# Graph layer kernel: product tiles in a new order, unused ranks taken from the row projection, edge sums joined to rank sums ahead of W2

## The chip, the cores and the metric

The kernel runs on one core of a Trainium2 chip. The metric is device time in microseconds (us) of the whole program, the median of several runs. The engines of the core work side by side: TensorE (PE in the profile; its weight loads are PEld), VectorE (DVE), ScalarE (ACT), GpSimd (POOL) and SyncE (SP), which here issues the DMA transfers. Each takes its own instructions in order and waits for others by semaphores.

## The reference

128 graphs of 128 nodes with 64 features, two layers. `h` is the layer norm of `x` with negative values set to zero.

```
mask = adj > 0
h1   = relu(h @ W1a [row j] + (h[j] - h[k]) @ W1b + b1)     # for each pair j, k; 192 hidden units
hm   = sum over k of mask[j, k] * h1[j, k, :]
x    = x + hm @ W2 + deg * b2                               # layer 0
x    = x + (adj @ h) @ W.T                                  # layer 1, h of the new x
```

With `A = h(W1a+W1b)+b1` and `C = h W1b`, one pair gives `relu(A[j] - C[k])`. The mask keeps about an eighth of the pairs, so most of the work of the dense sum is for nothing.

## The kernel before

**Tiling.** Four graphs are a group; 32 groups run one after another. The neighbours k of a row are cut in four quarters q of 32, and in each quarter a row's neighbours get ranks 0 to 5 (`D = 6`). `S` is one-hot: rank, neighbour, row. A product of the stacked projections `k3` with `S3` fetches, for each row and rank, `-C[k]`, and a second product with `id3` adds `A[j]`. The projections are split in three bf16 parts, which lie on 96 rows (3 x 32). The few neighbours beyond rank 5 of a quarter ("edges", `ov`) are gathered one by one into at most 128 edge slots (`R`, `RT`, `S2`, `X`).

The 192 hidden units are split: the first 128 (`C0`) use relu(v) = (v + |v|)/2, so DVE sums |v| straight out of PSUM into `hm0` (line 761), the linear part goes through the mask and the projections in `edge_sum`, and `w2h` is W2/2. The last 64 (`C1`) take relu on ACT into `T` (line 771), and POOL adds the 24 ranks up into `hm1` (lines 784 to 786).

**Unused ranks.** A rank that a row doesn't use fetches nothing, so its value is `A[j]` itself. What these add must be taken off again: `pre_ra` computes |A| and relu(A) with the hidden units as rows (`ra0`, `ra1`), `pre_pads` the number `np0` of used minus all ranks of each row, on all partitions, and POOL multiplies them. `edge_sum` and `edge_sum1` add the result to the edge sums (`u0`, `u1`). `post0` puts `u0`, both halves of `hm0`, `u1` and `hm1` through W2.

**Jobs.** A group takes 24 jobs, t = 0 to 23. A job fills one PSUM tile of the pool `g` (three buffers, shared with `pp` and `pr`) by products (`fill`) and drains it (`drain`): kind 0 has the first 128 units of one graph, 64 rows j (`jh`) and two quarters (`qp`), and is drained by DVE; kind 1 has the last 64 units of two graphs, one in each half of the columns, and is drained by ACT. The order is four jobs of kind 0, two of kind 1, repeated.

**What runs around the jobs.** Three tables say after which job a piece of other work is put out: `OWN` for the group of the jobs, `BEHIND` for the group before (its output), `AHEAD` for the next (its preparation). TensorE keeps this order exactly (`mm`, `tp`); within it, the other engines' instructions are placed by the framework. The pieces' small products use a second PSUM pool `m` with two buffers.

AHEAD makes, for the next group: `adjT` and `maskT` (pre_adj, t=2), the ranks `qs` (pre_rank, t=4) and from them the six planes of `S` and twelve transfers into `S3` (pre_slots, t=4), the projections `ca` and the row's part of the output `e` (pre_proj, twice), and twelve transfers of `ca` into `k3` (pre_stack). All transfers go through SP's queue in program order: `S3`, `k3`, the output of the group before, then the next loads. `S` has one buffer, `S3`, `k3` and `ca` two.

A job with `qp` 0 reads the quarters q = 0 and 1 of `S3` and `k3`, with `qp` 1 the quarters 2 and 3; q = 3 is the last one transferred.

Of the kernel before, what the change touches and what calls it, by code (L numbers as in the profile page):

```python
# [150 lines left out]
def kernel(  # L151
# [26 lines left out]
    nc = tc.nc  # L178
# [30 lines left out]
    with ExitStack() as main:  # L209
# [15 lines left out]
        ident = const.tile([P, P], F32, tag="ident", name="ident")  # L225
        make_identity(nc, ident)
        identb = const.tile([P, P], BF16, tag="identb", name="identb")
        nc.vector.tensor_copy(identb, ident)
# [12 lines left out]
        nc.vector.memset(oneb, 1.0)  # L241
        moneb = const.tile([P, P], BF16, tag="moneb", name="moneb")
        nc.vector.memset(moneb, -1.0)

# [31 lines left out]
        b1c = const.tile([P, 1], F32, tag="b1c", name="b1c")  # L276
        b1d = const.tile([P, 1], F32, tag="b1d", name="b1d")
        bias = const.tile([P, H + O], F32, tag="bias", name="bias")
        nc.vector.memset(w2bd, 0.0)
        nc.vector.memset(wl1, 0.0)  # L280
        for p in range(2):
            s = slice(p * F, (p + 1) * F)
            nc.scalar.dma_start(wa2[s, :], W1[0:F, :])
            nc.scalar.dma_start(wb2[s, :], W1[F : 2 * F, :])
            nc.scalar.dma_start(w2bd[s, p, :], W2[C0:H, :])
            nc.scalar.dma_start(wl1[s, s], W)
            nc.scalar.dma_start(b1d[s, :], b1[C0:H].unsqueeze(1))
        nc.scalar.dma_start(w2a, W2[0:C0, :])
# [137 lines left out]
        def pre_count(g):  # L426
            d = groups[g]

            pd = mtile(f"pd{g}")
            for b in range(G):  # L430
                mm(
                    pd[:, b : b + 1], d["maskT"][:, b, :], oneb[:, 0:1], start=True, stop=True
                )
                mm(
                    pd[:, G + b : G + b + 1], d["ov"][:, b, :], oneb[:, 0:1], start=True, stop=True
                )
            d["dn"] = grp.tile([P, 2, G], F32, tag="dn", name=f"dn{g}")
            nc.vector.tensor_copy(d["dn"].rearrange("j t b -> j (t b)"), pd[:, 0 : 2 * G])  # L438
            d["nb"] = tmp.tile([P, G], BF16, tag="nb", name=f"nb{g}")
            nc.vector.tensor_copy(d["nb"], d["dn"][:, 1])  # L440

        def pre_pads(g):
            d = groups[g]
            pn = mtile(f"pn{g}")
            for t, w in (("maskT", oneb), ("ov", moneb)):
                mm(
                    pn, w, d[t].rearrange("k b j -> k (b j)"), start=t == "maskT", stop=t == "ov"
                )
            d["np0"] = grp.tile([P, G, N], F32, tag="np0", name=f"np0{g}", bufs=1)
            nc.scalar.activation(  # L450
                d["np0"].rearrange("p b j -> p (b j)"), pn, AF.Copy, bias=-float(Q * D)
            )
            nc.gpsimd.tensor_tensor(d["ra0"], d["ra0"], d["np0"], ALU.mult)
            for p in range(2):
                s = slice(p * C1, (p + 1) * C1)
                nc.gpsimd.tensor_tensor(  # L456
                    d["ra1"][s], d["ra1"][s], d["np0"][s, 2 * p : 2 * p + 2], ALU.mult
                )

        def pre_proj(g, r):  # L460

            d = groups[g]
            if r == 0:

                d["ca"] = grp.tile([P, 3, 2, G, H], BF16, tag="ca", name=f"ca{g}")
                d["e"] = grp.tile([P, G, O], F32, tag="e", name=f"e{g}", bufs=3)
            pp = gtile(f"pp{g}_{r}")
# [28 lines left out]
        def pre_stack(g):  # L496
# [3 lines left out]
            for q in range(Q):  # L500
                for part in range(3):
# [3 lines left out]
                    )  # L505

        def pre_ra(g):
            d = groups[g]
            d["ra0"] = grp.tile([P, G, N], F32, tag="ra0", name=f"ra0{g}")
            d["ra1"] = grp.tile([P, 2, N], F32, tag="ra1", name=f"ra1{g}")  # L510
            halves = [slice(p * F, (p + 1) * F) for p in range(2)]
            pr = gtile(f"pr{g}")
            for p, s in enumerate(halves):
                mm(
                    pr[:, p, 0 : 2 * N].rearrange("h (r n) -> h r n", r=2),
                    wab[s, 0:C0], d["hT"][s], start=True, stop=True,
                )
            for p, s in enumerate(halves):
                mm(
                    pr[s, p, 2 * N : 4 * N].rearrange("h (r n) -> h r n", r=2),  # L520
                    wab[s, C0:H], d["hT"][s], start=True, stop=True,
                )
            nc.scalar.activation(
                d["ra0"].rearrange("h (p r) n -> h p (r n)", p=2), pr[:, :, 0 : 2 * N],
                AF.Abs, bias=b1c,
            )
            for p, s in enumerate(halves):
                nc.scalar.activation(
                    d["ra1"][s].rearrange("h r n -> h (r n)"),
                    pr[s, p, 2 * N : 4 * N], AF.Relu, bias=b1d[s],  # L530
                )

# [82 lines left out]
        def edge_sum(g):  # L615
# [3 lines left out]
            for b in range(G):  # L619
                o = ph[:, b * N : (b + 1) * N]  # L620
                mm(
                    o, d["X"][:, b, 0:C0], d["RT"][:, b, :], start=True, stop=False
                )
                for i in range(3):
# [5 lines left out]
            nc.vector.tensor_tensor(  # L630
                d["u0"], ph.rearrange("h (b j) -> h b j", b=G), d["ra0"], ALU.add
            )

        def edge_sum1(g):
            d = groups[g]
            ph = mtile(f"pe1{g}")
            for b in (0, 2, 1, 3):
                p, r = b // 2, b % 2
                mm(
                    ph[p * C1 : (p + 1) * C1, r * N : (r + 1) * N], d["X"][:, b, C0:H],  # L640
                    d["RT"][:, b, :], start=True, stop=True,
                )
            d["u1"] = tmp.tile([P, 2, N], F32, tag="u1", name=f"u1{g}", bufs=1)
            nc.vector.tensor_tensor(
                d["u1"], ph[:, 0 : 2 * N].rearrange("h (r j) -> h r j", r=2), d["ra1"], ALU.add
            )


        def post0(g):
            d = groups[g]  # L650
            py = mtile(f"py{g}")
            d["py"] = py
            for i, t in enumerate((d["u0"], d["hm0"][:, 0], d["hm0"][:, 1])):
                for p in range(2):
# [6 lines left out]
            w = w2bd.rearrange("h p o -> h (p o)")  # L661
            for i, t in enumerate(("u1", "hm1")):
                mm(
                    py[:, 0 : 2 * N], w, d[t].rearrange("h r j -> h (r j)"),
                    start=False, stop=i == 1, skip_group_check=True,
                )
            d["ys"] = tmp.tile([P, 2, N], F32, tag="ys", name=f"ys{g}")
# [50 lines left out]
        class Job:  # L718
# [108 lines left out]
        for g in range(NG):  # L827
            if g + 1 < NG:
                load(g + 1)
            for t in range(T):  # L830
# [46 lines left out]
```

## Time and profile before

| | |
|---|---|
| median of 3 runs | 1076.84 us (1076.46 to 1078.69) |
| the profiled execution | 1076.04 us, of which the span of the profile 1074.3 us |
| TensorE's granted clock | 0.987 |
| DVE: `hm` sums of kind 0 (L761) | 469.8 us busy, 949 ns each |
| POOL: sums of `T` (L784) | 442.1 us busy |
| TensorE: `g` from `S`, and from `id` | 383.4 and 381.3 us |
| ACT: `T` (L771) | 202.9 us busy, 805 ns each |
| transfers into `S3` | 384 of 192 KB, 4.0 us from issue to landing |
| transfers into `k3` | 384 of 96 KB, 2.2 us |

In the profile "out<-in" gives the tiles that an instruction writes and reads, with numbers left out: `g` are the product tiles, `pe` the sums of edge_sum and edge_sum1, `py` those of post0, `pp` the projections, `pr` and `pn` the products of pre_ra and pre_pads, `pq` the ranks, `px` the edge gather, `hm`, `u`, `T`, `S`, `k` the SBUF tiles named above. Line 181 and 184 are the helpers through which all products go, so products are told apart by their tiles. `96*64` is the shape of the weights: 96 rows, 64 columns; a number behind is the shape of the output. An fp32 product shows as two instructions. Matmuls overlap, so their durations add up to more than the time they take.

### The profile page before, as it was taken

The page shows a single profiled execution, that of the slowest core. Times are in us where ns is not written, and L with a number is a line of the kernel's source. Part 1 is how long each engine was busy: PE and PEld are TensorE (multiplying, and loading weights), DVE is VectorE, ACT ScalarE, POOL GpSimd, SP SyncE. Part 2 cuts the span into 40 slices and gives each one's busy share as a digit, 9 for nine tenths or more (in the row PEclk, how much of TensorE's full clock was granted, in tenths as well). Part 3 has the DMA queues.
Part 4 walks back from the last instruction along what each step waited for, and adds up shares of the span by engine and source line. Part 5 has one row for each costly group of instructions (what it writes and reads, how often), then busy time and mean ns, then how long its engine had stood idle before and what let it go on. Part 6 is the DMA issues. An engine that isn't in the chain of part 4 may idle for free.

```text
span 1074.3 us, 27146 instructions
## 1 busy us (share of the span) xinstructions
PE 1035.5 (96%) x10438; PEld 731.8 (68%) x10438; DVE 843.3 (79%) x1955; ACT 684.1 (64%) x1473; POOL 717.6 (67%) x810
## 2 busy tenths in 40 slices
PE   3699999999999999999999999999999999999995
PEld 1477776777677677677677677677777777667773
DVE  5468888878888878887877888877888887888763
ACT  4366666676666677666667666667666667666652
POOL 1377666777666687666686766677766677666674
PEclk9799999999999999999999999999999999999998
DMA  4456655456655456655456655445665545664420
GB/s 104 114 138 144 140 126 115 112 130 149 138 125 124 111 120 153 141 124 134 102 118 147 143 131 130 114 112 138 144 142 125 115 114 127 146 141 109 108 66 13
DMA packets 89062, 132.29 MB, mean 123 GB/s; under 512 B 47584, under 2 KB 64352, under 8 KB 88928
## 3 DMA queue, kind: packets, MB, share of 16 engines
q1 hardware_dynamic: 87552, 130.08, 53.0%
q8 instruction: 84, 1.38, 0.5%
q10 hardware_dynamic: 1376, 0.43, 0.2%
q14 instruction: 50, 0.41, 0.1%
HBM read 13.01 MB, written 4.19 MB: 16 GB/s over the span
## 4 chain that ended last, share of the span: by engine, by line
PE 93%; DVE 2%; SPq 2%; DMA 1%; ACT 1%; POOL 1%; issue 0%; ACTq 0%; POOLq 0%; DVEq 0%
PE g L181 49%; PE pe L181 7%; PE pp L181 7%; PE py L181 7%; PE px L181 6%; PE pr L181 3%; PE po L181 2%; PE pga L181 2%; PE pn L181 2%; PE pt L184 1%; PE pj L181 1%; PE pgq L181 1%; PE pq L181 1%; SPq L407 1%; DVE S L401 1%; PE pty L184 1%
## 5 line engine op out<-in xcount | busy, mean ns | idle before, releaser
L761 DVE TENSOR_REDUCE hm<-g 128x64 f32<-128x768 f32 x512 | 469.8, 949 | 115.7 <-PE g L181 113.5
L784 POOL TENSOR_TENSOR T<-T 128x768 f32<-128x768 f32 (+2 forms) x384 | 442.1, 1151 | 144.4 <-ACT T L771 126.8
L181 PEld LDWEIGHTS <-k 96*128 96x128 bf16 (+1 forms) x6144 | 408.5, 103 | 150.7 <-issue 37.2
L181 PE MATMUL g<-S,k 96*128 96x384 bf16 (+1 forms) x2048 | 383.4, 331 | 6.3 <-DMA k<-ca 5.1
L181 PE MATMUL g<-id,k 96*128 96x192 bf16 (+1 forms) x4096 | 381.3, 246 | 0.0
L771 ACT ACTIVATE T<-g 128x768 f32<-128x768 f32 x256 | 202.9, 805 | 25.4 <-PE g L181 23.4
L494 POOL TENSOR_TENSOR ca<-rest,ca 128x768 bf16<-128x768 f32 x64 | 105.0, 1642 | 170.5 <-ACT ca L493 161.1
L401 DVE TENSOR_SCALAR S<-qs 128x512 bf16<-128x512 bf16 x192 | 116.5, 675 | 3.0 <-issue 0.5
L483 ACT ACTIVATE ca<-pp 128x768 bf16<-128x768 f32 x64 | 51.3, 801 | 102.9 <-PE pp L181 99.0
L181 PE MATMUL pe<-RT,X 128*128 128x128 f32 (+1 forms) x512 | 79.4, 299 | 0.0
L493 ACT ACTIVATE ca<-rest 128x768 bf16<-128x768 f32 x64 | 53.7, 840 | 25.1 <-DVE rest L485 25.1
L181 PE MATMUL pp<-wp,hT 64*128 64x448 f32 x256 | 67.8, 607 | 1.9 <-DVE dn L438 1.9
L485 DVE TENSOR_TENSOR rest<-pp,ca 128x768 f32<-128x768 f32 x64 | 59.9, 936 | 4.5 <-ACT ca L483 4.5
L181 PEld LDWEIGHTS pe<-RT,X 128*128 128x128 f32 (+1 forms) x512 | 52.1, 164 | 9.8 <-issue 5.2
L668 ACT ACTIVATE ys<-py 128x256 f32<-128x256 f32 x32 | 12.3, 383 | 65.8 <-PE py L181 65.8
L456 POOL TENSOR_TENSOR ra<-ra,np 64x256 f32<-64x256 f32 x64 | 51.6, 806 | 2.4
L181 PE MATMUL px<-ca,S 128*128 128x192 bf16 x384 | 53.0, 247 | 0.0
L181 PE MATMUL px<-ca,R 128*128 128x192 bf16 x384 | 52.6, 246 | 0.0
L181 PEld LDWEIGHTS <-oneb 128*128 128x128 bf16 x192 | 13.5, 97 | 56.1 <-issue 56.1
L352 ACT ACTIVATE h<-x,mra,rsa 128x64 f32<-128x64 f32 x128 | 48.8, 435 | 3.7 <-DVE mra L350 2.2
L612 ACT ACTIVATE X<-px 128x256 f32<-128x256 f32 x64 | 24.5, 383 | 38.7 <-PE px L181 34.9
L181 PEld LDWEIGHTS <-R 128*128 128x128 bf16 x512 | 43.6, 98 | 7.9 <-issue 0.6
(130 smaller groups left out, 1425.0 us busy)
## 6 DMA issues: line engine op xcount, KB each, us to landing
S<-S SPq DMA_DIRECT2D x384, 192.0 KB, 4.0
k<-ca SPq DMA_DIRECT2D x384, 96.0 KB, 2.2
adj<-in_adj_dram SPq DMA_DIRECT2D x32, 256.0 KB, 2.8
x<-in_x_dram SPq DMA_DIRECT2D x32, 128.0 KB, 2.7
out_dram<-ot SPq DMA_DIRECT2D x32, 128.0 KB, 2.0
wa<-in_L_gnn_W_dram ACTq DMA_DIRECT2D x2, 48.0 KB, 2.8
wb<-in_L_gnn_W_dram ACTq DMA_DIRECT2D x2, 48.0 KB, 3.1
bias<-in_L_gnn_b_dram ACTq DMA_DIRECT2D x1, 96.0 KB, 4.1
```

What stands on the lines that cost most here:

```text
L181: return tc.keep_in_program_order(nc.tensor.matmul(*args, **kw))
L352: nc.scalar.activation(to(b), src[:, b, :], AF.Relu, bias=mr[:, b : b + 1], scale=rs[:, b : b + 1])
L401: nc.vector.tensor_scalar(d["S"][:, i, :], d["qs"].rearrange("k b j -> k (b j)"), float(i) + BIG, None, ALU.is_equal,)
L456: nc.gpsimd.tensor_tensor(d["ra1"][s], d["ra1"][s], d["np0"][s, 2 * p : 2 * p + 2], ALU.mult)
L483: nc.scalar.activation(parts[0], x, AF.Copy)
L485: nc.vector.tensor_tensor(rest, x, parts[0], ALU.subtract)
L493: nc.scalar.activation(parts[1], rest, AF.Copy)
L494: nc.gpsimd.tensor_tensor(parts[2], rest, parts[1], ALU.subtract)
L612: nc.scalar.activation(d["X"][:, r::2, 0:C0], pxv[:, :, 0:C0], AF.Abs)
L761: nc.vector.tensor_reduce(d["hm0"][:, qp, b, js], self.gt[:, :, 0:ND].rearrange("h i (d j) -> h j i d", d=D), AX.XY, ALU.add, apply_absolu ...
L771: nc.scalar.activation(d[key][:, qp].rearrange("h (i d) j -> h i d j", i=2), self.gt[:, :, 0:ND].rearrange("h i (d j) -> h i d j", d=D), A ...
L784: nc.gpsimd.tensor_tensor(t[:, 0:n], t[:, 0:n], t[:, n : 2 * n], ALU.add)
```

## The change

The products of `pre_ra` and `pre_pads` go, and what hangs on them. In their place `pre_proj` scales |A| and relu(A), which it has in PSUM with the rows j as partitions, by the number of unused ranks `ns` of each row, one activation for each graph and part (`z`); `edge_sum` and `edge_sum1` take `z` off by a product with minus the identity, in the same PSUM sum as the edges. The edge sums are then added to one half of `hm0` and to `hm1` on DVE, where `ra0` and `ra1` were added before, so the five operands of `post0` become three: the other half of `hm0`, `u0` and `u1`. The jobs come in runs of four or eight of one kind, and the three tables are laid out anew: among other moves, edge_sum and edge_sum1 go from OWN t=11 and t=9 (their own group's jobs) to BEHIND t=1 and t=4 (the next group's), edge_x to OWN t=10 and t=21, pre_proj to t=9 and t=10.

```diff
+        mident = const.tile([P, P], F32, tag="mident", name="mident")
+        nc.vector.tensor_scalar(mident, ident, -1.0, None, ALU.mult)
...
-            d["maskT"] = grp.tile([P, G, N], BF16, tag="maskT", name=f"maskT{g}")
+            d["maskT"] = grp.tile([P, G, N], BF16, tag="maskT", name=f"maskT{g}", bufs=3)
...
+            d["ns"] = grp.tile([P, G], F32, tag="ns", name=f"ns{g}")
+            nc.vector.scalar_tensor_tensor(
+                d["ns"], d["dn"][:, 1], float(Q * D), d["dn"][:, 0], ALU.add, ALU.subtract
+            )
...
-        def pre_pads(g):
...
             nc.scalar.activation(parts[0], x, AF.Copy)
+            for p in range(2):
+                b = 2 * p + r
+                for us, f in ((slice(0, C0), AF.Abs), (slice(C0, H), AF.Relu)):
+                    nc.scalar.activation(
+                        d["z"][:, b, us], x[:, p, 1, us], f, scale=d["ns"][:, b : b + 1]
+                    )
...
-        def pre_ra(g):
...
-                mm(
-                    o, d["X"][:, b, 0:C0], d["RT"][:, b, :], start=True, stop=False
-                )
+                mm(o, d["X"][:, b, 0:C0], d["RT"][:, b, :], start=True, stop=False)
+                mm(o, d["z"][:, b, 0:C0], mident, start=False, stop=False)
...
-                d["u0"], ph.rearrange("h (b j) -> h b j", b=G), d["ra0"], ALU.add
+                d["u0"], ph.rearrange("h (b j) -> h b j", b=G), d["hm0"][:, 0], ALU.add
...
+            for i, (l, m) in enumerate((("X", "RT"), ("z", None))):
+                for b in (0, 2, 1, 3):
+                    p, r = b // 2, b % 2
+                    mm(
+                        ph[p * C1 : (p + 1) * C1, r * N : (r + 1) * N], d[l][:, b, C0:H],
+                        d[m][:, b, :] if m else mident, start=i + r == 0, stop=i == 1,
+                        skip_group_check=True,
+                    )
...
-                d["u1"], ph[:, 0 : 2 * N].rearrange("h (r j) -> h r j", r=2), d["ra1"], ALU.add
+                d["u1"], ph[:, 0 : 2 * N].rearrange("h (r j) -> h r j", r=2), d["hm1"], ALU.add
...
-            for i, t in enumerate((d["u0"], d["hm0"][:, 0], d["hm0"][:, 1])):
+            for i, t in enumerate((d["hm0"][:, 1], d["u0"])):
...
-            5: (pre_hT,),
-            6: (pre_count,),
-            8: (lambda g: pre_proj(g, 0),),
-            9: (lambda g: pre_proj(g, 1), pre_stack,),
-            13: (pre_edge_a,),
+            6: (pre_hT, pre_count,),
+            9: (lambda g: pre_proj(g, 0),),
+            10: (lambda g: pre_proj(g, 1), pre_stack, pre_edge_a,),
             14: (pre_place,),
             20: (pre_edge_b,),
-            22: (pre_edge_d,),
-            23: (pre_ra, pre_pads, pre_edge_c,),
+            23: (pre_edge_d, pre_edge_c,),
         }
         OWN = {
-            3: (lambda g: edge_x(g, 0),),
-            5: (lambda g: edge_x(g, 1),),
-            9: (edge_sum1,),
-            11: (edge_sum,),
+            10: (lambda g: edge_x(g, 0),),
+            21: (lambda g: edge_x(g, 1),),
         }
         BEHIND = {
-            5: (post0,),
-            7: (post1,),
-            18: (post2,),
-            19: (post3,),
-            23: (post4,),
+            1: (edge_sum,),
+            4: (edge_sum1,),
+            6: (post0,),
+            8: (post1,),
+            15: (post2,),
+            17: (post3,),
+            20: (post4,),
         }
-        T = 24
+
+        ORDER = []
+        for r in range(2):
+            for jh in range(2):
+                ORDER += [(0, b, jh, qp) for b in (r, 2 + r) for qp in range(2)]
+                if jh == 0:
+                    ORDER += [(1, r, h, qp) for h in range(2) for qp in range(2)]
+        T = len(ORDER)
...
-                i, k = divmod(t, 6)
-                r, jh = divmod(i, 2)
-                k, qp = divmod(k, 2)
-                job = Job(g, 1, r, jh, qp) if k == 2 else Job(g, 0, 2 * k + r, jh, qp)
+            for t, args in enumerate(ORDER):
+                job = Job(g, *args)
```

More of the change, by code (lines that the diff above doesn't have):

```diff
@@ L241 @@
         nc.vector.memset(oneb, 1.0)
-        moneb = const.tile([P, P], BF16, tag="moneb", name="moneb")
-        nc.vector.memset(moneb, -1.0)
         upper = const.tile([P, P], F32, tag="upper", name="upper")
@@ L276 @@
         b1c = const.tile([P, 1], F32, tag="b1c", name="b1c")
-        b1d = const.tile([P, 1], F32, tag="b1d", name="b1d")
         bias = const.tile([P, H + O], F32, tag="bias", name="bias")
@@ L286 @@
             nc.scalar.dma_start(wl1[s, s], W)
-            nc.scalar.dma_start(b1d[s, :], b1[C0:H].unsqueeze(1))
         nc.scalar.dma_start(w2a, W2[0:C0, :])
@@ L438, in pre_count @@
             nc.vector.tensor_copy(d["dn"].rearrange("j t b -> j (t b)"), pd[:, 0 : 2 * G])
+            d["ns"] = grp.tile([P, G], F32, tag="ns", name=f"ns{g}")
+            nc.vector.scalar_tensor_tensor(
+                d["ns"], d["dn"][:, 1], float(Q * D), d["dn"][:, 0], ALU.add, ALU.subtract
+            )
             d["nb"] = tmp.tile([P, G], BF16, tag="nb", name=f"nb{g}")
             nc.vector.tensor_copy(d["nb"], d["dn"][:, 1])
-        def pre_pads(g):
-            d = groups[g]
-            pn = mtile(f"pn{g}")
-            for t, w in (("maskT", oneb), ("ov", moneb)):
-                mm(
-                    pn, w, d[t].rearrange("k b j -> k (b j)"), start=t == "maskT", stop=t == "ov"
-                )
[L449 to L458, printed above, removed]
         def pre_proj(g, r):
@@ L465, in pre_proj @@
                 d["ca"] = grp.tile([P, 3, 2, G, H], BF16, tag="ca", name=f"ca{g}")
+                d["z"] = grp.tile([P, G, H], F32, tag="z", name=f"z{g}")
                 d["e"] = grp.tile([P, G, O], F32, tag="e", name=f"e{g}", bufs=3)
@@ L505, in pre_stack @@
                     )
-        def pre_ra(g):
[L508 to L531, printed above, removed]
         def pre_edge_a(g):
@@ L620, in edge_sum @@
                 o = ph[:, b * N : (b + 1) * N]
-                mm(
-                    o, d["X"][:, b, 0:C0], d["RT"][:, b, :], start=True, stop=False
-                )
+                mm(o, d["X"][:, b, 0:C0], d["RT"][:, b, :], start=True, stop=False)
+                mm(o, d["z"][:, b, 0:C0], mident, start=False, stop=False)
                 for i in range(3):
@@ L636, in edge_sum1 @@
             ph = mtile(f"pe1{g}")
[L637 to L642, printed above, removed]
+            for i, (l, m) in enumerate((("X", "RT"), ("z", None))):
[6 more added lines that the diff above has]
+                    )
             d["u1"] = tmp.tile([P, 2, N], F32, tag="u1", name=f"u1{g}", bufs=1)
             nc.vector.tensor_tensor(
-                d["u1"], ph[:, 0 : 2 * N].rearrange("h (r j) -> h r j", r=2), d["ra1"], ALU.add
+                d["u1"], ph[:, 0 : 2 * N].rearrange("h (r j) -> h r j", r=2), d["hm1"], ALU.add
             )
@@ L661, in post0 @@
             w = w2bd.rearrange("h p o -> h (p o)")
[L662 to L666, printed above, removed]
+            mm(
+                py[:, 0 : 2 * N], w, d["u1"].rearrange("h r j -> h (r j)"),
+                start=False, stop=True, skip_group_check=True,
+            )
             d["ys"] = tmp.tile([P, 2, N], F32, tag="ys", name=f"ys{g}")
@@ L829 @@
                 load(g + 1)
-            for t in range(T):
-                i, k = divmod(t, 6)
-                r, jh = divmod(i, 2)
-                k, qp = divmod(k, 2)
-                job = Job(g, 1, r, jh, qp) if k == 2 else Job(g, 0, 2 * k + r, jh, qp)
+            for t, args in enumerate(ORDER):
+                job = Job(g, *args)
                 job.fill()
```

## The prediction

> **What bounds the kernel now.** I read the page first, then TensorE's timeline of one period, then the same stretch on SP, DVE and POOL.
>
> ```profile
> PE 1035.5 (96%) x10438; PEld 731.8 (68%) x10438; DVE 843.3 (79%) x1955; ACT 684.1 (64%) x1473; POOL 717.6 (67%) x810
> PE 93%; DVE 2%; SPq 2%; DMA 1%; ACT 1%; POOL 1%; issue 0%; ACTq 0%; POOLq 0%; DVEq 0%
> ```
>
> TensorE is busy 96% of the span and carries 93% of the chain that ended last. By its timeline the groups start every 31.96 us (519.77, 551.73): 30 equal periods between a start-up (first product at 34.35) and a tail. I call the 24 places in a period t=0 to t=23. TensorE is in program order and pipelined, so what an item costs is the distance from its start to the next start, not the duration shown:
>
> ```profile
> 505.48 0.49 PE L181 MATMUL pe<-RT,X 128*128 128x128 f32 x2
> 505.81 0.33 PE L181 MATMUL pe<-maskT,ca 128*128 128x128 bf16 x3
> 505.97 0.44 PE L181 MATMUL pe<-RT,X 128*128 128x128 f32 x2
> 506.25 0.33 PE L181 MATMUL pe<-maskT,ca 128*128 128x128 bf16 x3
> ...
> 517.89 1.28 PE L181 MATMUL pr<-hT,wp 64*128 64x256 f32 x8
> 519.11 0.39 PE L181 MATMUL pn<-maskT,oneb 128*128 128x512 bf16 x1
> 519.33 0.38 PE L181 MATMUL pn<-ov,moneb 128*128 128x512 bf16 x1
> 519.55 0.39 PE L181 MATMUL prt<-identb,R 128*128 128x128 bf16 x4
> ...
> 526.89 0.65 PE L181 MATMUL py<-u,w2h 128*64 128x256 f32 x4
> 527.37 1.03 PE L181 MATMUL py<-hm,w2h 128*64 128x256 f32 x8
> 528.33 0.70 PE L181 MATMUL py<-u,w2bd 128*128 128x256 f32 x2
> 528.87 0.59 PE L181 MATMUL py<-hm,w2bd 128*128 128x256 f32 x2
> 529.30 0.38 PE L184 MATMUL ph<-ident,h 128*128 128x128 f32 x2
> ```
>
> An fp32 128x128x128 product costs 0.28 us (505.97 to 506.25), `pr` 1.22, `pn` 0.44, and the four blocks of `py` 0.48, 0.97, 0.54 and 0.43. A job costs 0.655.
>
> Under TensorE a second chain is almost as long, SP's queue:
>
> ```profile
> 524.70 0.39 PE L181 MATMUL pq<-maskT,triq 128*128 128x512 bf16 x1
> 526.57 3.72 DVE L401 TENSOR_SCALAR S<-qs 128x512 bf16<-128x512 bf16 x6
> 527.01 3.80 POOL L784 TENSOR_TENSOR T<-T 128x768 f32<-128x768 f32 x3 [1.54 <-ACT T L771]
> 530.32 10.64 SPq L407 DMA_DIRECT2D S<-S  x12
> 541.07 8.35 SPq L502 DMA_DIRECT2D k<-ca  x12
> 550.41 0.39 SPq L715 DMA_DIRECT2D out_dram<-ot  x1
> ```
>
> The rank product `pq` (t=4) leads to `qs`, to six DVE comparisons (`S`, done 530.29), to twelve `S3` transfers, and behind them in the same queue twelve `k3` transfers. The next group needs all of it at once: its second job (t=1) reads slot q=3, the last transfer. By the trace's DMA records the last landing comes 20.8 us after the last `S` (mean of periods 2 to 30, 20.0 to 22.1), and q=3 is used 1.4 us (0.6 to 2.2) after it landed. So the profile shows no wait here, but the chain has only 1.4 us to spare in 31.96.
>
> ```profile
> 530.30:541.00 10.70, 10.68 (x110) 7.37 (x108) 10.15 (x36) 6.31 (x12) 5.35 (x6) 1.00 0.84 183
> 541.00:549.40 8.40, 8.40 (x101) 6.05 (x100) 7.33 (x13) 7.29 (x19) 6.75 (x9) 1.00 0.70 169
> ```
>
> Last two columns: DMA share 0.84 and 0.70, GB/s 183 and 169 in those two stretches. They are transfers at work, so their length will not shrink for TensorE's sake.
>
> **What the Trainium skill says.** "TensorEngine Tiling (Array Packing)", Key Properties: changing the tiling mode drains TensorE. The trace agrees: the second half of a 64-column job costs 0.33 before another such job (510.87 to 511.20) and 0.43 before a 128-row, 128-column product (524.27 to 524.70), so 0.10 us a change. "GPSIMD Engine Reference", Specifications: its SBUF interface is shared with VectorE and contends with DVE's two-port modes. The trace agrees: an `S` comparison takes 0.29 us while POOL rests and 1.90 when POOL's `T` sum is running (527.19). "ScalarE: Activation LUTs", What ACT_TABLE_LOAD costs: a per-partition pointer adds about 93 ns; the 128-wide `et` with one takes 0.39 here.
>
> **The change on TensorE, per period.** Removed: `pr` 1.22, `pn` 0.44, one of three `w2h` blocks 0.48 and one of two `w2bd` 0.43: 2.57. Added: in edge_sum four fp32 products with `mident`, 4 x 0.277 = 1.11; in edge_sum1 four half-width ones. `pe1` itself costs 0.48 without a mode change (1043.22 to 1043.70), so 0.48 more: 1.59. Mode changes: I count about 24 before, two of them inside `pr`; of the other 22, the new order leaves 12 (around t=4 to 7 and 16 to 19, at `pq`, after post0's 64-column part, and around each `pp`). 10 x 0.1 = 1.0. Sum: 31.96 - 2.57 + 1.59 - 1.0 = 30.0 us, if nothing else waits.
>
> **ACT, POOL, DVE.** ACT loses `ra` and `np` (2.2 us a period), gains eight `z`: four 128-wide at 0.39, four 64-wide at 0.33, 2.9 less 0.8 overlap. They stand between the two `ca` copies, where ACT waits 0.74 us for DVE's `rest` anyway; they also hold the `pp` buffer, but DVE's `rest` and `e` hold it as long. POOL loses 2.9 us of `ra` products. DVE gains one 4-wide `ns`, 0.16. DVE's flow is about 26 us a period: enough for 30. None of these sets the period by its sum.
>
> **What the moves do to SP's chain.** This is the step that decides. edge_sum goes from t=11 to t=1 and edge_sum1 from t=9 to t=4, both in front of `pq`, which stays at t=4; edge_x(0), which was in front at t=3, leaves. From the q=3 product in t=1 to the end of `pq`: before 0.49 rest of the job + 0.655 + `pt` 0.44 + 0.655 + `px` 1.09 + 0.78 + 0.39 = 4.50 (the trace: 520.59 to 525.09). After: 0.49 + edge_sum 2.94 (1.83 + 1.11) + 0.655 + 0.44 + 0.755 + 0.68 + edge_sum1 0.96 + 0.1 + 0.39 = 7.41, 2.9 later. Then `pq`'s end to the last `S`: 5.2 before; ACT no longer has the first `T` copy in the way of `qs`, so 4.9; POOL's `T` sum still follows the second 64-column job at once and still falls on the comparisons. Then 20.8 to the last landing; 0.3 to 0.4 of this is a wait of `k` on POOL, of which I take half away: 20.65. Then 0.14 from landing to product (39.91 to 40.05 at the start). Loop: 7.41 + 4.9 + 20.65 + 0.14 = 33.1 us. TensorE's 30.0 doesn't matter; it will stand at t=1 until the last `k3` is there. Bounds: if half of POOL's collision goes, 32.5; if the comparisons lose a further turn or landing is at its worst every second time, 33.8.
>
> **Sum.** 30 periods x (33.1 - 31.97) = +34. The first period has no work of a group behind and loses edge_x ahead of `pq`: about -1.8. The tail about -0.5. 1074.3 + 31.7 = 1106 span, with the 1.74 around it 1107.8; the median of the runs shown lies 0.8 above the profiled run: 1108.5. I say 1108.
>
> **Rivals.**
> (A, forecast, 0.70) SP's chain sets the period: 32.5 to 33.8, so 1090 to 1130. For it: 1.4 us of room against 2.6 us of delay (2.9 - 0.3), and a period that wants to shrink. It decides from the point where `pq` moves by more than the room.
> (B, 0.17) `S` gets through before POOL starts (six at 0.21 are 1.3 us instead of 3.7), so SP's loop is about 31, and TensorE is held by buffers instead. `pd` now follows `py` directly with two `m` buffers and waits for the copy `ys`, 0.4. The third product tile after `pp` r=1 needs that buffer: copy 0.8, `rest` 0.86 and `e` 0.38 with hand-overs take 2.3 us, and only two jobs (1.31) lie beside it, where before 64-column jobs and edge_sum did; eight jobs drained by DVE at 0.87 follow each other there, so 1.0 to 1.5. P = 30.0 + 0.4 + 1.0 to 1.5, about 31.5: 1060. Against: the `T` sum follows `pq` by the same distance as before.
> (C, 0.13) Nothing waits: 30.0 to 30.4, and a shorter first period: about 1017. Against: it needs the landings 3 us sooner than the queue has delivered them in any period.
>
> **How the numbers follow.** Low 1050 takes in most of B, high 1130 the top of A; C and the ends are left out, about 0.18. A alone: 1090 to 1130. About 0.2% is what a measurement of this kernel can tell from no change: faster by more takes C and most of B, 0.25; within it 0.03; slower 0.72.
>
> **What would show it.** Right: TensorE waits named "DMA k" at the second job of each group, 2 to 3 us each; groups 33 us apart; `pq` 2.9 us later after t=1; SP never long without an issue except ahead of `S`. TensorE's summed busy time falls by some 50 us in either case: `pr`, `pn` gone, fewer changes of mode. Wrong: groups 30 to 31 us apart, no DMA among TensorE's releasers, and `S` done within 2 us; or waits of `g` on DVE `e` and `hm` larger than those on `k`.

## The result and the profile after

The changed kernel takes 1114.99 us (median of 4 runs, 1112.84 to 1116.37) beside 1076.65 us for the kernel before on the same chip (4 runs, 1076.09 to 1078.69): a ratio of 1.035, 95% interval 1.033 to 1.037. The profiled execution took 1112.84 us, its span is 1111.1 us. It is slower by 38 us, where 31 were forecast.

The page of the kernel after: busy time by engine, then the chain that ended last, by engine and by line.

```profile
PE 995.4 (90%) x10438; PEld 747.0 (67%) x10438; DVE 837.1 (75%) x1987; ACT 672.5 (61%) x1601; POOL 626.1 (56%) x714
...
PE 36%; ACT 18%; DVE 16%; SPq 16%; DMA 7%; POOL 4%; issue 3%; ACTq 0%; DVEq 0%
PE g L181 17%; SPq L495 16%; PE pe L181 10%; DVE hm L728 8%; DMA k<-ca 6%; ACT ca L486 5%; PE py L181 4%; POOL ca L487 4%; ACT et L514 3%; ACT h L350 3%; ACT z L474 3%; DVE rest L478 2%; ACT ca L470 2%; DVE stb L336 1%; DVE sta L336 1%
```

TensorE's busy time fell by 40 us, as the change's products promise, and POOL's by 92. But the span grew by 37: TensorE carried 93% of the chain before and carries 36% now. The rest is a relay through ACT, DVE, SP's queue of `k3` transfers (L495), DMA and POOL. What is missing from these largest shares is to be noted: no `S`, and no `S3` transfer (L405).

The waits of TensorE after (what waited, for what: us in total, times, longest):

```profile
PE g L181 <- DMA k<-ca: 32.0, 35, 2.5
PE g L181 <- DVE hm L728: 19.0, 32, 1.2
PE g L181 <- DVE e L482: 9.8, 30, 1.4
PE g L181 <- ACT T L738: 9.1, 30, 0.7
```

About once a period a product waits for a `k3` transfer. The chain of waits over one period shows what made that transfer late (start, length, piece of the chain):

```profile
501.24 2.15 DMA k<-ca
503.39 0.09 issue
503.48 0.65 PE g L181 x5
...
519.24 0.86 DVE hm L728
520.10 0.87 DVE rest L478
520.98 0.02 issue
521.00 0.84 ACT ca L486
521.84 0.33 ACT h L350
522.17 0.69 ACT ca L470
522.87 0.93 ACT z L474 x4
523.79 1.16 ACT et L514 x4
524.95 0.66 ACT h L350 x2
525.60 0.74 ACT ca L486
526.35 0.07 issue
526.41 1.65 POOL ca L487
528.06 0.02 issue
528.08 0.51 SPq L495
...
533.72 2.20 DMA k<-ca
535.92 0.14 issue
536.06 0.65 PE g L181 x5
```

The relay ends where it began, at the second job of a group, 32.6 us later. POOL ends the third part of `ca` at 528.06, and 0.02 us later SP issues a transfer that had waited for it, the third of twelve; nine more follow it, and the last lands at 535.92. The Trainium skill says where such a wait is spent, in "DMA: Bandwidth & Descriptors", Anatomy of one DMA — SWDGE (gpsimd) path: the transfer engines wait for no semaphore, the issuing engine does. The trace agrees for SP: what waits there holds all that SP has behind it. SP's waits for POOL over the whole run, and its timeline in that stretch:

```profile
SPq L495 <- POOL ca L487: 32.0, 30, 1.1
...
514.49 10.13 SPq L405 DMA_DIRECT2D S<-S  x12
524.72 9.59 SPq L495 DMA_DIRECT2D k<-ca  x12
```

The `S3` transfers were through at 524.6. So `S` isn't what the last `k3` transfer waited for.

One loop of the queue, from the q = 3 product of one group to that of the next, by the trace's instruction and DMA records (mean of periods 2 to 30; the smallest and largest in brackets where it matters):

| us | before | forecast | after |
|---|---|---|---|
| q = 3 product to end of `pq` | 4.50 | 7.41 | 7.14 |
| `pq` to the last `S` | 5.22 | 4.9 | 3.99 |
| `S3` issues, and the gap to `k3` | 10.44 | | 10.43 |
| first `k3` issue to the end of the last | 8.60 | | 9.93 (8.88 to 11.3) |
| end of that issue to landing | 1.79 | | 1.61 |
| last `S` to last landing | 20.83 | 20.65 | 21.97 |
| landing to the product that uses it | 1.44 (0.62 to 2.21) | 0.14 | 0.12 (0.05 to 0.14) |
| period | 31.98 | 33.1 | 33.22 |

30 times 1.24 us is 37 us: the whole difference lies in the period. The last row but one says that the last landing sets it, as forecast. But `S` came 1.2 us sooner than forecast, and the `k3` transfers took 1.3 us longer. Two errors cancelled.

### The profile page after: what moved, and what is told of

Its sections match the earlier page's. It is cut to its first block, busy times and chain, and to the rows that moved or that the text cites. A ratio compares the mean times of both kernels' runs of the same rounds, so it can differ in the third digit from the quotient of the medians.

```text
span 1111.1 us, 27179 instructions
## 1 busy us (share of the span) xinstructions
PE 995.4 (90%) x10438; PEld 747.0 (67%) x10438; DVE 837.1 (75%) x1987; ACT 672.5 (61%) x1601; POOL 626.1 (56%) x714
## 4 chain that ended last, share of the span: by engine, by line
PE 36%; ACT 18%; DVE 16%; SPq 16%; DMA 7%; POOL 4%; issue 3%; ACTq 0%; DVEq 0%
PE g L181 17%; SPq L495 16%; PE pe L181 10%; DVE hm L728 8%; DMA k<-ca 6%; ACT ca L486 5%; PE py L181 4%; POOL ca L487 4%; ACT et L514 3%; ACT h L350 3%; ACT z L474 3%; DVE rest L478 2%; ACT ca L470 2%; DVE stb L336 1%; DVE sta L336 1%
## 5 line engine op out<-in xcount | busy, mean ns | idle before, releaser
L181 PEld LDWEIGHTS <-k 96*64 96x64 bf16 (+1 forms) x6144 | 419.9, 103 | 234.8 <-issue 100.1
L181 PE MATMUL g<-S,k 96*64 96x384 bf16 (+1 forms) x2048 | 389.5, 330 | 77.5 <-DMA k<-ca 32.0
L399 DVE TENSOR_SCALAR S<-qs 128x512 bf16<-128x512 bf16 x192 | 93.5, 556 | 2.6
L181 PE MATMUL pe<-RT,X 128*64 128x128 f32 (+1 forms) x512 | 76.6, 289 | 0.0
L181 PE MATMUL pe<-mident,z 128*64 128x128 f32 (+1 forms) x512 | 70.0, 276 | 0.0
L474 ACT ACTIVATE z<-pp,ns 128x128 f32<-128x128 f32 (+1 forms) x256 | 65.9, 344 | 0.0
L596 DVE TENSOR_TENSOR u<-pe,hm 128x512 f32<-128x512 f32 x32 | 22.1, 692 | 53.3 <-PE pe L181 53.3
L181 PEld LDWEIGHTS pe<-mident,z 128*64 128x64 f32 (+1 forms) x512 | 55.0, 167 | 0.0
L181 PEld LDWEIGHTS pe<-RT,X 128*64 128x64 f32 (+1 forms) x512 | 54.2, 167 | 0.1
L350 ACT ACTIVATE h<-x,mrb,rsb 128x64 f32<-128x64 f32 x128 | 52.1, 438 | 0.4 <-DVE mrb L348 0.4
```

Of the source, the lines that this page charges most:

```text
L181: return tc.keep_in_program_order(nc.tensor.matmul(*args, **kw))
L350: nc.scalar.activation(to(b), src[:, b, :], AF.Relu, bias=mr[:, b : b + 1], scale=rs[:, b : b + 1])
L399: nc.vector.tensor_scalar(d["S"][:, i, :], d["qs"].rearrange("k b j -> k (b j)"), float(i) + BIG, None, ALU.is_equal,)
L474: nc.scalar.activation(d["z"][:, b, us], x[:, p, 1, us], f, scale=d["ns"][:, b : b + 1])
```

## The experiments

Three theories were tried. Theory 1: SP's queue is late because `S` is late. Theory 2: the third `k3` transfer waits for POOL's third part of `ca`, and holds the nine behind it. Theory 3: TensorE's product tiles are held too long by DVE's drains and `pp` (rival B). Each kernel is the kernel after with the edit shown, unless said otherwise; times are medians, ratios stand against the kernel before on the same chip, with the 95% interval.

**The ranks earlier.**

```diff
-            2: (pre_adj,),
+            0: (pre_adj,),
+            1: (pre_rank, pre_slots,),
             3: (pre_norm,),
-            4: (pre_rank, pre_slots,),
```

> pre_adj is put out after t=0 and pre_rank with pre_slots after t=1, so pq ends about 3.6 us sooner after the product that reads q=3, and the S3 transfers start that much sooner; nothing else moves. Theory 1 (the S queue: the twelve S3 transfers, late because edge_sum stands ahead of pq, push the k3 transfers back): the period falls from 33.2 to about 31.2 to 32, 1055 to 1080 us. Theory 2 (the third part: the third k3 transfer waits for POOL's last ca, and the nine behind it wait in the queue): the first two transfers go sooner, the third doesn't; 1110 to 1118 us.

Measured: 1108.18 us, ratio 1.028 [1.026, 1.030], period 33.01: far above the range of theory 1, 2 us below that of theory 2. `pq` ended 3.5 us after the q = 3 product, the last `S` 2.36 after that, so the queue got its work 5.3 us sooner than in the kernel after. The period fell by 0.2. Now SP stood 3.1 us without work ahead of `k3`, and the third transfer started 5.19 us after the first. Theory 1 falls.

**The `k3` transfers by part**, so that the four that need POOL's part come last.

```diff
-            for q in range(Q):
-                for part in range(3):
+            for part in range(3):
+                for q in range(Q):
```

> The same twelve k3 transfers, put out part by part instead of quarter by quarter, so that the four that need POOL's third part come last, 5 us after the first. Theory 1: the queue starts no sooner and is no shorter, 1112 to 1118 us. Theory 2: the wait of the third transfer, 3.2 us after the first where 1.3 would do, goes; the period falls by 1.2 to 1.9 until the product tiles held by DVE's eight drains are the next limit (31.5 to 32.0): 1062 to 1080 us.

Measured: 1084.86 us, 1.007 [1.005, 1.009], period 32.27. That is 5 us above the range of theory 2 and 27 below that of theory 1. Two lines change places and 30 of the 38 us are gone; TensorE's waits for the `k3` transfers fell from 32.0 us to 3.5, and SP no longer waits for POOL's `ca`. The third transfer starts 1.81 us after the first, against 3.17 in the kernel after (and 1.79 in the kernel before, where the wait thus costs next to nothing). The last landing now comes 0.39 us ahead of its use. Theory 2 holds, for the kernel after.

**The `et` activations later**, out of ACT's way between the two `ca` copies.

```diff
-            10: (lambda g: pre_proj(g, 1), pre_stack, pre_edge_a,),
+            10: (lambda g: pre_proj(g, 1), pre_stack,),
+            13: (pre_edge_a,),
```

> pre_edge_a after t=13, where the kernel before has it, instead of t=10: its four et activations (1.2 us) come behind the second ca copy of r=1 on ACT. Theory 1: 1112 to 1118 us. Theory 2: POOL's last ca comes up to 1.2 us sooner, the period falls by as much: 1080 to 1100 us.

Measured: 1095.21 us, 1.016 [1.015, 1.018], period 32.53. POOL's part ended 23.94 us after the q = 3 product, 0.76 sooner, and the period fell by 0.69, as theory 2 expected.

**`z` behind the third part.** The eight activations are moved from between the `ca` copies to behind POOL's subtraction.

```diff
             nc.scalar.activation(parts[0], x, AF.Copy)
-            for p in range(2):
...
             nc.gpsimd.tensor_tensor(parts[2], rest, parts[1], ALU.subtract)
+            for p in range(2):
```

> The z activations are put out behind the third part of ca, so ACT takes ca, ca, z instead of ca, z, ca; same work. Theory 1: 1112 to 1118 us. Theory 2, if z is what keeps ACT or DVE's rest from the second copy: 0.5 to 0.9 us a period sooner, 1088 to 1100 us; if DVE's drains and et keep it, no change.

Measured: 1237.73 us, 1.150 [1.148, 1.152], period 37.28 in the mean and 37.55 in most: a miss for every theory, and the largest effect of all. A line of TensorE's waits and one of the chain, then the windows of 1 us in one period (columns: length, then busy time of PE, PEld, DVE, ACT, POOL with counts, PEclk, DMA share, GB/s):

```profile
PE g L181 <- DVE hm L728: 88.4, 90, 1.5
...
567.49 1.21 DVE mrb L348
...
568.00:569.00 1.00, 0.80 (x8) 0.52 (x6) 1.00 (x6) 0.69 (x2) 0.67 (x1) 1.00 1.04 227
569.00:570.00 1.00, 0.12 (x1) 0.10 (x1) 1.00 (x2) 1.00 (x4) 0.00 (x0) 1.00 1.02 215
570.00:571.00 1.00, 0.70 (x6) 0.44 (x5) 1.00 (x3) 1.00 (x4) 0.00 (x0) 1.00 0.98 203
571.00:572.00 1.00, 0.00 (x1) 0.00 (x1) 1.00 (x3) 1.00 (x3) 0.25 (x1) 0.62 0.98 203
572.00:573.00 1.00, 1.00 (x5) 0.64 (x5) 0.81 (x1) 1.00 (x5) 1.00 (x1) 0.50 0.84 181
...
580.00:581.00 1.00, 1.00 (x14) 0.72 (x12) 0.00 (x0) 0.49 (x1) 1.00 (x1) 0.50 0.68 163
581.00:582.00 1.00, 1.00 (x14) 0.63 (x11) 0.00 (x0) 0.95 (x3) 0.92 (x2) 0.76 0.42 98
582.00:583.00 1.00, 1.00 (x11) 0.90 (x10) 0.56 (x1) 1.00 (x3) 0.84 (x3) 1.00 0.00 0
```

TensorE's first loss is small: its waits on DVE's `hm` for a free tile come to 88.4 us, where the four largest waits for a product in the kernel after came to 69.9. Two things make the drains later. `pp` is read to the end only behind the second `ca` copy, so its tile comes free later, and it is a third of the pool. And `mrb`, an instruction of 128x4 ahead of a drain on DVE, takes 1.19 us in the mean, 0.15 in the kernel after; POOL's subtraction, which starts sooner here, runs beside it. The two weren't tried apart.

But these waits lie close together, and then the granted clock falls to 0.50 for about 10 us, with TensorE busy throughout. The mean clock was 0.874 against 0.985. Two of the first periods, with 3.4 us at half clock, take 34.6 us; those with 10.2, 37.55. By these figures most of the 4.1 us by which the mean period grew goes with the half clock.

On the chain of theory 2 the edit did what was meant: POOL's part ended 23.99 us after the q = 3 product, 0.71 sooner. It gained nothing, since the landing now came 5.0 us ahead of its use.

**Both cures of theory 2.**

```diff
-            for q in range(Q):
-                for part in range(3):
+            for part in range(3):
+                for q in range(Q):
...
-            10: (lambda g: pre_proj(g, 1), pre_stack, pre_edge_a,),
+            10: (lambda g: pre_proj(g, 1), pre_stack,),
+            13: (pre_edge_a,),
```

> The two that helped, together: k3 transfers part by part, pre_edge_a after t=13. No transfer waits for POOL any more. If SP's queue is then the limit (theory 1 with the transfers' own times: 7.0 to pq, 4.0 to S, 10.3 S3, 7.6 to 8.4 k3, 1.7 landing, 0.1), the period is 30.8 to 31.6, 1040 to 1065 us. Theory 3 (product tiles held by DVE's eight drains in a row and by pp, about 2.8 us of stalls in a period over 29.25 us of TensorE work): 31.9 to 32.1, 1073 to 1083 us, with hardly a wait on k left.

Measured: 1078.17 us, 1.0015 [1.0006, 1.0024], period 32.04, with 0.21 us from landing to use: the range of theory 3. The order of `k3` and of `et` together undo what the change lost. Both ends nearly meet: TensorE's own period, often 31.67, and the queue's.

**All three edits**, the ranks earlier as well, so that nothing of the queue is near.

```diff
-            2: (pre_adj,),
+            0: (pre_adj,),
+            1: (pre_rank, pre_slots,),
...
-            for q in range(Q):
-                for part in range(3):
+            for part in range(3):
+                for q in range(Q):
...
+            13: (pre_edge_a,),
```

> The changed kernel with all three moves that were tried singly: ranks early, k3 part by part, pre_edge_a at 13. SP's chain has room of 3 us. Theory 3: what is left is stalls on product tiles, 31.5 to 31.9 in every period, 1062 to 1075 us. If the transfers still held r5: 30 to 31, 1025 to 1055 us.

Measured: 1077.27 us, 1.0005 [0.9996, 1.0013], period 32.18, nearly the same in every period, with 2.97 us from landing to use: 2 us above the range of theory 3, far above the other. TensorE's waits:

```profile
PE g L181 <- DVE hm L728: 28.3, 93, 0.7
PE g L181 <- DVE e L482: 12.4, 30, 0.4
...
PE pd L181 <- ACT ys L635: 7.6, 30, 0.3
```

With the queue out of the way TensorE still needs 32.2 us, though its work in a period is about 29 us by an estimate (a period of 33.43 us of the kernel after, 4.2 of stalls taken off). Three `hm` waits a period, one on `e`, one of `pd` on `ys`: these are the waits of theory 3, which is rival B. They would then be worth about 3 us a period, not the 1.4 to 1.9 that the rival gave them. It isn't one number for all places: the periods of the kernel with both cures in which the landing came well ahead took 31.67, those with `k3` by part alone 32.08. That the product tiles set these periods is read from the waits; the two edits that were to lift it, the next one and, further below, the old job order with the joins, both made the kernel slower.

**The projections among the 64-column jobs**, where ACT drains and DVE doesn't: ranks at t = 1, `hT` at 3, projections at t = 6 and 7, and the two edits of theory 2.

```diff
-            6: (pre_hT, pre_count,),
-            9: (lambda g: pre_proj(g, 0),),
-            10: (lambda g: pre_proj(g, 1), pre_stack, pre_edge_a,),
+            3: (pre_hT,),
+            4: (pre_count,),
+            6: (lambda g: pre_proj(g, 0),),
+            7: (lambda g: pre_proj(g, 1), pre_stack,),
+            13: (pre_edge_a,),
```

> Ranks after t=1, hT and counts after t=3 and 4, both pre_proj after t=6 and 7, in the run of jobs that ACT drains; k3 part by part; pre_edge_a at 13. SP's chain then has 4 us to spare, and the tiles of pp no longer lie between eight DVE drains. Theory 3: most of the 2.8 us of stalls goes, period 30.0 to 30.7, 1015 to 1040 us. If the eight drains hold TensorE without pp too: 31 to 32, 1045 to 1080 us.

Measured: 1137.89 us (1137.46 to 1138.37), 1.057 [1.055, 1.059], period 34.14: a miss. The landing had 7.7 us to spare. TensorE's waits name ACT and DVE:

```profile
PE pga L181 <- ACT h L350: 50.7, 64, 2.6
PE g L181 <- DVE hm L728: 29.4, 61, 0.8
PE g L181 <- ACT T L738: 14.7, 31, 0.5
```

ACT has the `T` copies in those places, and now the projections' copies and `z` too. The product of the layer's aggregation then waits for a late `h`, twice a period. That ACT's load there is the cause is read from these waits, not tried by itself.

**The arithmetic alone.** The kernel before, with its order, its tables and its five operands of `post0`; only `ra` and `np` are replaced by `z` and the product with `mident`. Nothing is joined ahead of W2.

```diff
-        def pre_pads(g):
...
+                        d["z"][:, b, us], x[:, p, 1, us], f, scale=d["ns"][:, b : b + 1]
...
-        def pre_ra(g):
...
+                mm(o, d["z"][:, b, 0:C0], mident, start=False, stop=False)
...
-            nc.vector.tensor_tensor(
-                d["u0"], ph.rearrange("h (b j) -> h b j", b=G), d["ra0"], ALU.add
-            )
+            nc.vector.tensor_copy(d["u0"], ph.rearrange("h (b j) -> h b j", b=G))
...
-            23: (pre_ra, pre_pads, pre_edge_c,),
+            23: (pre_edge_c,),
```

> The arithmetic alone: z in place of ra and np, in the order and at the places of the kernel before, u0 and u1 copied instead of added to, post0 with its five operands. TensorE: 1.66 us a period less, 1.34 more (z products measured at 0.224 and 0.11), one change of mode less: 31.5 instead of 31.96, 1060 to 1068 us, if the arithmetic is harmless and the moves alone cost. If z on ACT delays the third part by more than the 1.4 us of room: 1077 us or more.

Measured: 1070.46 us, 0.995 [0.994, 0.997], period 31.75: between the two ranges. Here too the third `k3` transfer comes late, 3.02 us after the first, and TensorE waits for it in most periods:

```profile
PE g L181 <- DMA k<-ca: 14.9, 23, 2.5
```

So `z` alone is enough to delay POOL's part (it ends 23.13 us after the q = 3 product; 21.29 before). Periods without that wait take 31.33.

**The same, with the `k3` transfers by part.**

```diff
-            for q in range(Q):
-                for part in range(3):
+            for part in range(3):
+                for q in range(Q):
```

> r7_z_only with the k3 transfers part by part. Theory 2: the waits on k that held r7 at 31.75 on average (31.33 in the periods without one) go; 31.33 to 31.4 throughout: 1055 to 1062 us. If the transfers themselves and not the third part held it: 1068 to 1072 us.

Measured: 1056.66 us (5 runs, 1056.51 to 1060.52), 0.983 [0.981, 0.984], period 31.36: the best of all, faster than both kernels. Busy time and chain by engine:

```profile
PE 1015.7 (96%) x10630; PEld 749.5 (71%) x10630; DVE 846.4 (80%) x1987; ACT 674.5 (64%) x1601; POOL 629.9 (60%) x714
...
PE 93%; DVE 2%; ACT 2%; DMA 1%; POOL 1%; SPq 1%; issue 0%; ACTq 0%; POOLq 0%; DVEq 0%
```

TensorE is the bound again, 20 us shorter than before, and the landing has 0.90 us to spare. Whether the order of `k3` alone would help the kernel before wasn't tried; its third transfer starts no later than here (1.79 and 1.77), so nothing speaks for it.

**The moves alone.** The kernel before with its arithmetic, and the jobs and tables of the kernel after; `pre_ra` and `pre_pads` stay at t = 23.

```diff
-            9: (edge_sum1,),
-            11: (edge_sum,),
+            10: (lambda g: edge_x(g, 0),),
+            21: (lambda g: edge_x(g, 1),),
         }
         BEHIND = {
-            5: (post0,),
+            1: (edge_sum,),
+            4: (edge_sum1,),
+            6: (post0,),
...
+                    ORDER += [(1, r, h, qp) for h in range(2) for qp in range(2)]
```

> The moves alone: jobs in runs and the new tables, with ra and np as before (put out after t=23) and post0 with five operands; nothing of z. TensorE's work 29.25 + 1.66 - 1.34 + 0.9 = 30.5 us a period. Theory 2: the third part is late by the places of pre_proj, et and the drains, without z's 0.9 us on ACT: period 32.3 to 33.5, 1085 to 1120 us. If the arithmetic (z) is what made the kernel slower: 30.5 to 31.5, 1030 to 1065 us.

Measured: 1205.77 us, 1.121 [1.119, 1.123], periods from 34.3 to 38.6: a miss, far above both ranges. POOL's part ended 24.56 us after the q = 3 product, nearly as late as in the kernel after (24.70), so the moves alone are enough for most of that delay. But it didn't set the period: the landing had 3.0 us to spare, and TensorE waited for tiles:

```profile
PE g L181 <- DVE hm L761: 50.4, 31, 1.7
PE g L181 <- DVE e L489: 19.7, 28, 1.6
```

These waits fall together after the second projection, and the granted clock then goes to 0.50 here as well (mean 0.936); periods at full clock take about 34.4 us, those with 10.2 us at half clock 38.2 to 38.6. So the moves cost and the arithmetic doesn't: on the old order the new arithmetic gains 6 us, on the new order the old one loses 129. This kernel also has `pr` in the pool of product tiles, which the kernel after hasn't, so the 129 us aren't a price of the moves in the kernel after.

**The old job order with the joins.** New arithmetic and joins, jobs in runs of four and two, edge sums behind t = 1 and 4, ranks at t = 1, `k3` by part; several other pieces change places too.

```diff
-                if jh == 0:
-                    ORDER += [(1, r, h, qp) for h in range(2) for qp in range(2)]
+                ORDER += [(1, r, jh, qp) for qp in range(2)]
...
-            6: (post0,),
-            8: (post1,),
+            5: (post0,),
+            7: (post1,),
```

> The new arithmetic with its joined sums (edge_sum after t=1 of the next group, ahead of it pre_adj, behind it the ranks), but jobs in the old order of four and two, pre_proj at 8 and 9, k3 part by part. Theory 3: with two ACT-drained jobs after every four the tiles come free; TensorE's work about 29.9 (four to six more changes of mode), period 30.0 to 30.6, 1015 to 1040 us. If the stalls come from elsewhere (m tiles, ACT): 31 or more, 1045 to 1080 us.

Measured: 1120.66 us, 1.041 [1.039, 1.043], period mostly 33.9: a miss. 6.5 us lay between landing and use; a product tile waited for ACT once a period, 1.3 us each, and the mean clock was 0.949. In 25 of 29 periods the clock was halved for 3.4 us; the four others took 32.27. TensorE's waits:

```profile
PE g L181 <- ACT T L738: 39.4, 31, 1.3
PE g L181 <- DVE e L482: 16.3, 31, 0.6
```

So most of this loss goes with the half clock. Even without it the period is near that of the kernel with all three edits (32.18), so the runs of eight aren't needed for a limit near 32 us. Which of the places makes it here wasn't tried.

**The join on POOL**, in the best kernel: POOL adds `u0` and `u1` to the rank sums after t = 2, `edge_x` goes to t = 5 and 7, and `post0` has three operands.

```diff
+        def join(g):
+            d = groups[g]
+            nc.gpsimd.tensor_tensor(d["u0"], d["u0"], d["hm0"][:, 0], ALU.add)
+            nc.gpsimd.tensor_tensor(d["u1"], d["u1"], d["hm1"], ALU.add)
...
-            for i, t in enumerate((d["u0"], d["hm0"][:, 0], d["hm0"][:, 1])):
+            for i, t in enumerate((d["hm0"][:, 1], d["u0"])):
...
-            3: (lambda g: edge_x(g, 0),),
-            5: (lambda g: edge_x(g, 1),),
+            5: (lambda g: edge_x(g, 0),),
+            7: (lambda g: edge_x(g, 1),),
```

> r9_z_part with the join of the change, but done by POOL (which has 2.9 us a period free since ra went) in two sums put out after t=2 of the next group, so that edge_sum and edge_sum1 stay with their own group; post0 has three operands; edge_x after t=5 and 7, behind pq. TensorE's work falls by 0.9 us: period 30.4 to 30.8 (SP's chain, 1.1 us sooner at pq, allows about 30), 1028 to 1045 us. If POOL's sums push the T sums or S back: 31 to 32, 1050 to 1075 us.

Measured: 1087.85 us, 1.010 [1.009, 1.012], period 32.41: a miss. Products worth about 0.9 us a period went, and the period grew by 1.1. One new wait stands out,

```profile
PE pty L184 <- DVE dn L436: 15.8, 29, 0.7
```

and stalls of 0.1 to 0.3 us at several tiles behind it. The two moves weren't tried apart; which of them costs stays open.

## Why the prediction was right, and where it was right by luck

**What bounds it, and TensorE's sum.** Right. TensorE's own work isn't the limit after: about 29 us a period, by the estimate above, where 30.0 was worked out (in part because a product with `mident` takes 0.22 us, 504.22 to 504.44, not 0.277). Its busy time fell by 40 us, against "some 50".

**The end.** Right: the last `k3` landing sets the period, 0.12 us ahead of its use, at 33.22 us where 33.1 was said. TensorE waits named "DMA k" at the second job are there, 0.9 us in the mean and 2.5 at most, shorter than the 2 to 3 expected, since the tiles held TensorE up as well and it came later to them.

**The delay of `pq`.** Right in kind, 7.14 for 7.41; again the smaller `mident` product. It isn't what decides: with `pq` 3.6 us earlier the kernel still takes 1108 us.

**The term "`pq`'s end to the last `S`": 4.9, measured 3.99.** It was assumed that the `T` sum falls on the comparisons as before. It does, but later: in the period shown they start 1.04 us after `pq` (1.48 before) and POOL 0.67 us after them (0.44 before), so that more of them pass in time; the six took 2.92 us for 3.72. The mean of one fell from 675 to 556 ns.

**The step that failed: "a wait of `k` on POOL, of which I take half away".** It grew to about 1.4 us (third transfer 3.17 us after the first; 1.81 unhindered). Nor was there anything to halve: in the kernel before the third transfer starts 1.79 us after the first, as soon as in the kernels where it needs nothing of POOL (1.77 and 1.81), so the 0.3 to 0.4 us read there cost no time. From the q = 3 product to the end of POOL's second third part of `ca` it is 24.70 us, 3.41 more than before; by the records:

| us, mean of periods 2 to 30 | before | after | more |
|---|---|---|---|
| q = 3 product to end of `pp`, second projection | 15.28 | 17.49 | 2.21 |
| to start of ACT's first `ca` copy | 0.30 | 1.23 | 0.93 |
| end of that copy to start of DVE's `rest` | 0.12 | 0.96 | 0.84 |
| end of `rest` to start of ACT's second copy | 0.26 | 0.71 | 0.45 |
| end of that copy to start of POOL | 1.12 | 0.08 | -1.04 |

The rows hold what the prediction looked at by engine and not along this chain. The projection stands one place later, behind the edge sums. ACT is still at work on the first projection. `z` was put at nothing because ACT "waits 0.74 us for DVE's `rest` anyway", but `rest` now starts at the end of `z`, so `z` pushes what was to hide it. And `et` and two `h` stand ahead of the second copy. The queue passed on only 1.40 us of delay to its first `k3` transfer, so POOL's part, which was 1.13 us behind that start, is now 3.14 behind. Freed of that wait, the queue's path is about 32.0 (32.27 less the 0.39, plus 0.12, in the kernel with `k3` by part).

**Rivals.** B stood hidden behind the queue: 31.7 to 32.2 us a period, for 31.5. Its waits are the named ones, `hm`, `e` and `ys`, and its stalls were priced about 1 us too low. At their true price it gives little or no gain. C, nothing waits, needed both B and the queue away; no run came near 30.4. The forecast's 31 us don't follow from its cause: with `S` as the only thing late, the kernel after would have come out near 1085 us, as with `k3` by part, or lower.

Shown by runs: the third part's wait (two cures, each by itself), that `S` isn't what is late, that another limit of 31.7 to 32.2 us a period stands behind the queue, and that the arithmetic gains in the old order. Argued only: that product tiles are this limit, how the stalls with `z` last begin, and why ACT's early projections and the join on POOL lose.

## What to carry to other kernels

When a chain ends in a queue, follow every input of every transfer in it to the engine that makes it, not only the first one: a queue served in order is as late as its latest early item, so let the transfers whose data come last stand last. Take a change's arithmetic and its moves apart before judging either: here the arithmetic was worth 20 us once one loop was turned round, and the moves cost more. Where several limits lie within about 1 us of each other (here 33.2, 32.2 and 32.0), removing one shows the next, and a forecast that names one should price the others with the same care.

## What the runs showed of the hardware

- **Short waits near each other, and then half the clock.** In the kernel with `z` last, TensorE was idle 0.52, 1.09 and 1.30 us between 566.8 and 572.0, and was then granted 0.50 for about 10 us while it had work throughout. The moves alone show the same after 1.68 and 0.66 us idle between 554.8 and 558.0. The Trainium skill, "TensorE: Matmul & The Clock Gate", Part 1: The HAM clock gate, says that the clock is halved after an idle window of about 3.4 us and comes back after a busy one. The traces agree on the one half, and the half clock lasts 3.4, 6.8 or 10.2 us in nearly all of these periods, one to three such windows. They differ in that the stretch before it was only about half idle. In the kernel after, with 0.9 us idle between 522 and 526, the clock stayed at 1.00. What share of idle time is enough wasn't tried.
- **DVE's comparisons take up to three times as long beside POOL's sums.** The six `S` comparisons take 1.30 us where POOL rests (ranks earlier), 2.95 in the kernel after, 3.76 in the best kernel; what differs beside them is where POOL's `T` sum starts. The `hm` sums, which read PSUM, take 0.95 us in the mean in all three.
- **The first `k3` transfers go out more slowly behind the `S3` transfers.** Without any wait for data the third is issued 1.8 us after the first there, and 1.23 us after it where SP had stood idle before (all three edits).
